# Loading the band tiles of an involution kernel two bands at a time, with smaller rings beside them

## The chip, the cores and the metric

The kernel runs on one core of one Trainium2 chip. The metric is the device time of one execution in microseconds. A core has five engines that run side by side, each in its own order: TensorE (PE in the profile; its weight loads are shown apart as PEld), VectorE (DVE), ScalarE (ACT), GpSimd (POOL) and SyncE (SP). POOL and SP here mostly issue transfers, which the core's 16 DMA engines carry out.

## What is computed

For a batch of 32 images of 256 channels and 32 x 32 pixels, two residual layers:

```
# layer 0
x = x + conv3x3_quantised(group_norm(x)) + bias      # operands and result rounded to fp16
# layer 1: involution, 16 groups of 16 channels, 7 x 7 taps
n = group_norm(x)
y = relu(scale * (w1 @ n) + shift)                   # 64 channels
w = w2 @ y + b2                                      # [16 groups, 49 taps, 32, 32]
x = x + sum over taps k of w[g, k, h, w] * n[g, c, h + k_h - 3, w + k_w - 3]
```

The taps of layer 1 are different at every pixel and are themselves computed. The kernel does the last sum on TensorE: for a block of input pixels it multiplies their channel values by a banded matrix that holds, in each input pixel's row, that pixel's weight in every output pixel in reach.

## The kernel before

**Bands.** An image is cut into K = 4 bands of TR = 8 rows, a band into 2 sides of JC = 16 columns. The 128 partitions of a band tile are the 8 x 16 pixels of one side; each side has its own stretch of 3,528 floats, a window of 22 output columns of 160 floats (16 groups x 10 rows) and a pad. `sums(b, m)` (L508) multiplies one side of one band (m runs over the 8 of an image) with the pixels in 64 matmuls of 64 x 32 (L522) into the PSUM tile `acc`, and `add_windows` (L530) adds the result to x on DVE (L538).

**How a band gets its layout.** `weights(b, r0)` (L403) makes the taps of four image rows on PE (`pw`, L411). `evict` (L424, L435) adds the bias on DVE and writes them into `w_sb`, a ring of RING = 32 output rows in SBUF; `ring_pieces` (L437) cuts the write where the ring or the image ends. `scatter(b, k, part)` (L465) writes the eight rows of a band from `w_sb` to the DRAM array `wd` in seven transfers, one for each horizontal tap (L476): runs of 640 bytes, four transfers in part 0 and three in part 1. `load_bands(b, k)` (L478) reads them back, shifted by a row's offset, into one of NBAND = 3 band tiles: 16 transfers, one for each column j of a side, each with 8 partitions and the two sides of them, runs of 4,512 bytes where nothing is cut off (L497). Columns 0 and 1 go through SP, the other 14 through POOL. Side 1 is stored mirrored, so that both sides have their image edge at j = 0; `backwards` (L277) turns the pixel order of side 1 in xn and y to match. In column 15 the two sides' runs lie side by side and become one.

**Fronts.** `front(b)` (L284) is a generator that does everything before an image's sums: group norm of layer 0 (sums on ACT, L214; grouping on DVE, L224 to L230; mean and squares on ACT), the 3 x 3 convolution in 16-bit (`pc`, L332, 18 matmuls for each of 4 output units), its rounding and residual on DVE (L346, L348), group norm of layer 1, the normalised xn (L273), the 1 x 1 convolution `py` (L377) with its activation to y (L388), and the transposes `pt` of xn (L396), whose copies on ACT (L400) fill one of NPIX = 6 pixel buffers for each band. `py` and `pt` share one PSUM buffer, the single one of the pool `ps_m`. There are two y buffers.

**Order.** The order is written out by hand: the loop at L556 runs over steps n, 16 to an image, and every engine executes its instructions in the order in which the loop emits them. A front advances by one `yield` in each step, except at `yield LATER`, which lets the other fronts go first within the step. Relative to the first sums of image b (step 0), its front starts at step FRONT = -56; `py` comes at step -20, `pt` and copy of its four bands at -14, -12, -10 and -8; `weights` come at every second step from -LEAD = -18; the two parts of a scatter one and two steps after the weights that complete its rows; the load of band k at step 4k - 9; the sums of m at step 2m, their addition to x a step later. About three fronts are in progress at any time, so an engine's queue interleaves several images. Counted within a repeating batch of 16 steps, -20 is the same place as -4, -56 as -8. Within a step the order is: fronts (the oldest image first), sums, addition, store, weights, scatters, load of x, band loads.

The waits between engines follow from the tiles: who overwrites a tile waits for those who read it.

## Time and profile before

| | us |
|---|---|
| three runs | 1348.22, 1356.12, 1360.93 |
| their median | 1356.12 |
| the profiled execution | 1344.24 |
| its span, first to last instruction | 1342.5 |

| engine | busy, us | share | instructions |
|---|---|---|---|
| PE matmul | 1253.6 | 93% | 27,648 |
| PE weight load | 763.7 | 57% | 27,648 |
| DVE | 818.8 | 61% | 2,539 |
| ACT | 733.3 | 55% | 1,731 |
| POOL | 1014.4 | 76% | 1,818 |

The page also shows the traffic: 361.85 MB in all, 270 GB/s over the span. SP's queue moved 229.38 MB and took 56.8% of the 16 engines' time, POOL's 128.28 MB and 33.9%. SP issues 896 scatters of 160 KB, 64 loads of x and 64 stores of 512 KB and 256 band loads; POOL issues 1,792 band loads of mostly 70.5 KB, 4.6 us from issue to landing in the median.

How to read it: the five engines' times overlap, so they don't add up. A share near 100% says only that an engine may be the limit. The chain of waits goes back from the last instruction to what released it, so its shares do add up. A row of a group gives busy time and mean ns of an instruction, then the idle time of its engine just before, with who ended most of it; the idle time of an engine that isn't the limit costs nothing. A matmul's time is modelled. The first sums start at 87.7 us.

### The profile page before, as it was taken

The page shows a single profiled execution, that of the slowest core. Times are in us where ns is not written, and L with a number is a line of the kernel's source. Part 1 is how long each engine was busy: PE and PEld are TensorE (multiplying, and loading weights), DVE is VectorE, ACT ScalarE, POOL GpSimd, SP SyncE. Part 2 cuts the span into 40 slices and gives each one's busy share as a digit, 9 for nine tenths or more (in the row PEclk, how much of TensorE's full clock was granted, in tenths as well). Part 3 has the DMA queues.
Part 4 walks back from the last instruction along what each step waited for, and adds up shares of the span by engine and source line. Part 5 has one row for each costly group of instructions (what it writes and reads, how often), then busy time and mean ns, then how long its engine had stood idle before and what let it go on. Part 6 is the DMA issues. An engine that isn't in the chain of part 4 may idle for free.

```text
span 1342.5 us, 65799 instructions
## 1 busy us (share of the span) xinstructions
PE 1253.6 (93%) x27648; PEld 763.7 (57%) x27648; DVE 818.8 (61%) x2539; ACT 733.3 (55%) x1731; POOL 1014.4 (76%) x1818
## 2 busy tenths in 40 slices
PE   5899999999999999999999999999999999999665
PEld 2356566565555655556655556666555566556454
DVE  3466666565666665656665666766666666666442
ACT  5775656455656556556545655655556564553300
POOL 9067878777787778777778787788777877788785
PEclk9999999999999999999999999999999999999987
DMA  6089999999999999999999999999999999999995
GB/s 228 11 237 295 271 293 293 279 266 281 272 286 282 291 285 270 283 263 280 293 282 283 270 288 282 293 297 296 281 288 275 277 284 290 271 281 266 278 274 166
DMA packets 360724, 361.85 MB, mean 270 GB/s; under 512 B 75056, under 2 KB 304752, under 8 KB 359152
## 3 DMA queue, kind: packets, MB, share of 16 engines
q1 hardware_dynamic: 278512, 229.38, 56.8%
q0 software_dynamic: 81920, 128.28, 33.9%
q8 instruction: 220, 3.60, 1.1%
q14 instruction: 72, 0.59, 0.1%
HBM read 176.60 MB, written 180.76 MB: 266 GB/s over the span
## 4 chain that ended last, share of the span: by engine, by line
PE 60%; DMA 23%; POOL 7%; issue 3%; ACT 3%; DVE 2%; SPq 1%; POOLq 0%; DVEq 0%; ACTq 0%
PE pc L332 25%; PE acc L522 19%; DMA band<-wd 17%; PE pw L411 11%; POOL band L497 7%; DMA wd<-w_sb 6%; PE pt L396 3%; PE py L377 3%; ACT junk L214 1%; SPq L476 1%; DVE w_sb L435 1%; DMA x<-in_x 1%; ACT xn L273 0%; SPq L497 0%; ACT xq L273 0%
## 5 line engine op out<-in xcount | busy, mean ns | idle before, releaser
L497 POOL DMA_DIRECT2D band<-wd x1792 | 980.3, 549 | 315.7 <-DMA band<-wd 182.0
L435 DVE TENSOR_TENSOR w_sb<-pw,late_sb 128x224 f32<-128x224 f32 (+7 forms) x1280 | 330.4, 322 | 419.5 <-PE pw L411 419.2
L332 PE MATMUL pc<-xq,wq 128*128 128x496 f16 (+3 forms) x2304 | 535.2, 379 | 20.3 <-ACT xq L273 18.3
L522 PE MATMUL acc<-band,pixels 64*32 64x190 f32 (+1 forms) x16384 | 426.6, 332 | 51.8 <-DMA band<-wd 42.7
L522 PEld LDWEIGHTS acc<-band,pixels 64*32 64x32 f32 x16384 | 304.7, 107 | 159.7 <-issue 81.1
L332 PEld LDWEIGHTS <-wq 128*128 128x128 f16 x2304 | 206.7, 98 | 316.1 <-issue 102.7
L411 PE MATMUL pw<-late_sb,y 64*32 64x224 f32 (+1 forms) x8192 | 288.9, 333 | 10.8 <-issue 9.4
L538 DVE TENSOR_TENSOR x<-acc,x 128x380 f32<-128x380 f32 (+1 forms) x512 | 262.0, 512 | 32.2 <-PE acc L522 23.2
L411 PEld LDWEIGHTS pw<-late_sb,y 64*32 64x32 f32 x8192 | 186.5, 106 | 38.1 <-issue 21.0
L400 ACT COPY pixels<-pt 128x512 f32<-128x512 f32 x128 | 73.7, 576 | 228.6 <-PE pt L396 228.6
L214 ACT ACTIVATE junk<-x 128x512 f16<-128x512 f32 (+1 forms) x192 | 146.4, 763 | 14.7 <-DVE x L348 12.2
L214 ACT ACTIVATE junk<-x,mean 128x1024 f16<-128x1024 f32 x128 | 147.1, 1149 | 4.3
L245 ACT ACTIVATE s<-back,eps 128x2 f32<-128x2 f32 x64 | 18.9, 296 | 178.6 <-DVE back L230 178.6
L346 DVE TENSOR_SCALAR q<-pc 128x512 f16<-128x512 f32 x128 | 87.2, 681 | 17.6 <-PE pc L332 17.6
L273 ACT ACTIVATE xn<-x,off,rstd 128x512 f32<-128x512 f32 x128 | 96.2, 800 | 0.0
L348 DVE SCALAR_TENSOR_TENSOR x<-q,early_sb,x 128x512 f32<-128x512 f16 x128 | 94.2, 736 | 0.3
L396 PEld LDWEIGHTS pt<-ident,xn 128*128 128x128 f32 x512 | 63.9, 142 | 26.3 <-issue 2.5
L396 PE MATMUL pt<-ident,xn 128*128 128x128 f32 x512 | 78.0, 275 | 0.1
L273 ACT ACTIVATE xq<-x,off,rstd 128x1024 f16<-128x1024 f32 x64 | 75.7, 1227 | 0.0
L235 ACT ACTIVATE mean<-back 128x2 f32<-128x2 f32 x64 | 12.6, 196 | 101.4 <-DVE back L230 101.4
L377 PE MATMUL py<-xn,early_sb 128*64 128x512 f32 x256 | 62.2, 606 | 0.9 <-ACT xn L273 0.9
L224 DVE STREAM_TRANSPOSE across<-sums 128x32 f32<-128x32 f32 x128 | 26.3, 205 | 33.6 <-ACT junk L214 32.4
(40 smaller groups left out, 369.3 us busy)
## 6 DMA issues: line engine op xcount, KB each, us to landing
wd<-w_sb SPq DMA_DIRECT2D x896, 160.0 KB
band<-wd POOLq DMA_DIRECT2D x1664, 70.5 KB, 4.6
x<-in_x SPq DMA_DIRECT2D x64, 512.0 KB
out<-x SPq DMA_DIRECT2D x64, 512.0 KB
band<-wd POOLq DMA_DIRECT2D x128, 60.5 KB, 4.6
band<-wd SPq DMA_DIRECT2D x128, 50.5 KB
band<-wd SPq DMA_DIRECT2D x128, 40.5 KB
band<-in_w SPq DMA_DIRECT2D x2, 1152.0 KB
```

Source lines behind the costliest of these rows:

```text
L214: nc.scalar.activation(junk[:, n0:n1], src[:, h, n0:n1], func, bias=bias, accum_out=self.sums[:, i : i + 1])
L273: nc.scalar.activation(dst, src, AF.Identity, bias=self.off[:, one], scale=self.rstd[:, one])
L332: nc.tensor.matmul(pc.rearrange("p (r c) -> p r c", c=W)[:, r0 - nt * RT : r1 - nt * RT, c0:c1], wq[:, kh, k, mh * P : (mh + 1) * P], xq[: ...
L346: nc.vector.tensor_scalar(q, pc, F16_MAX, -F16_MAX, ALU.min, ALU.max)
L348: nc.vector.scalar_tensor_tensor(xt[:, mh, cols], q, bias_sb[:, mh : mh + 1], xt[:, mh, cols], ALU.add, ALU.add)
L377: nc.tensor.matmul(py[i * CR : (i + 1) * CR], w1_sb[:, kh, :], px[:, :, i], start=kh == 0, stop=kh == CH - 1,)
L396: nc.tensor.transpose(pt[:, i, h * P : (h + 1) * P], xn[:, h, (m + i) * P : (m + i + 1) * P], ident)
L411: nc.tensor.matmul(pws[i][t * TW : (t + 1) * TW, : dj.stop - dj.start, r], y_sb[b % 2][half, (r0 // 2 + r) * W : (r0 // 2 + r + 1) * W], w ...
L435: nc.vector.tensor_tensor(to, of[:, :, d0:d1], bias[:, :, d0:d1], ALU.add)
L497: queue.dma_start(to, src)
L522: nc.tensor.matmul(at[t * TW : (t + 1) * TW, h, :, f - top : l - top], px[p, a, v * GC : v * GC + TW], of[:, :, a, f - top : l - top, v], ...
L538: nc.vector.tensor_tensor(x_at, of, x_at, ALU.add)
```

## The change

- `wd` is laid out as two rows of bands: the eight rows of bands 2q and 2q + 1 lie side by side, 70 columns instead of 38 for each row (SP, ROW).
- `load_bands(b, q, queue, columns)` loads a pair of bands. A transfer of column j takes all four sides of the pair, 32 runs, where no side needs a cut (j = 3 to 12); for the six columns at the edges, side 0 and side 1 have a transfer of their own with 16 runs. Because neighbours now lie side by side in `wd`, what lies beyond an image's edge is cut off in the transfer (cut, end). POOL issues 18 (BY_GPSIMD) and SP four (BY_SYNC) for each pair, in the order of the lists, POOL at step 8q - 9 and SP at 8q - 8.
- The three band tiles become two tiles of a pair each, `halves`, of 13,632 floats; the windows of neighbouring sides follow each other in it.
- Side 1 is no longer mirrored; `backwards` goes.
- One y instead of two; LEAD is 20, so that the first `weights` come in the step of `py`.
- RING is 20 rows instead of 32. `evict` then writes in pieces where the ring ends, and a scatter whose eight rows cross the ring's end becomes two sets of seven transfers of four rows.
- NPIX is 5. HELD moves the copies from `pt` to the pixel buffers: the third comes a step after its `pt`, the fourth three steps after it.
- The scratch for descriptors of POOL's transfers is halved (SCRATCH).

```diff
-ROW = S * WPIX
+BOTH = 2
+SP = BOTH * W + 2 * PAD1
+ROW = SP * WPIX
+STEP = WINC * WB + PAD
+UNITS = BOTH * SIDES
+HALF = (UNITS - 1) * STEP + (JC + PAD1) * WB + PAD
+BY_SYNC = ((0, 0), (15, 1), (1, 0), (14, 1))
+BY_GPSIMD = (
+    (8, None), (4, None), (0, 1), (15, 0), (9, None), (5, None), (1, 1), (14, 0), (10, None),
+    (6, None), (2, 1), (13, 0), (11, None), (7, None), (2, 0), (13, 1), (12, None), (3, None),
+)
+NPIX = 5
+RING = 20
+SCRATCH = 2048
-NBAND = 3
-BY_SYNC = (0, 1)
-ORDER = (0, 4, 8, 12, 2, 5, 9, 13, 3, 1, 6, 10, 14, 7, 11, 15)
-NPIX = 6
-RING = 32
-SCRATCH = 4096
-LEAD = 18
+LEAD = 20
+HELD = (0, 0, 1, 3)
...
-    y_sb = [const.tile([P, N // 2], F32, name=f"y_{i}") for i in range(2)]
-    bands = [const.tile([P, SIDES, WINC * WB + PAD], F32, name=f"band_{i}") for i in range(NBAND)]
-    for t in bands[CH:]:
-        nc.gpsimd.memset(t, 0.0)
+    y_sb = const.tile([P, N // 2], F32, name="y")
+    halves = [const.tile([P, HALF], F32, name=f"bands_{i}") for i in range(2)]
+    parts = [halves[0][:, : HALF // 2], halves[0][:, HALF // 2 :]]
+    zeros = halves[1]
+    for i in range(8):
+        nc.gpsimd.memset(zeros[:, i * HALF // 8 : (i + 1) * HALF // 8], 0.0)
-    wd = dram.tile([H, S, WPIX], F32, name="wd")
+    wd = dram.tile([K // BOTH, TR, SP, WPIX], F32, name="wd")
...
             yield
             to = xn[:, h].rearrange("p (k d r j) -> p d k r j", d=SIDES, r=TR, j=JC)
             at = xt[:, h].rearrange("p (k r d j) -> p d k r j", d=SIDES, r=TR, j=JC)
-            gn.apply(h, [(to[:, 0], at[:, 0]), (to[:, 1], backwards(at[:, 1]))])
+            gn.apply(h, [(to[:, d], at[:, d]) for d in range(SIDES)])
         yield from stages(2)
 
         py = ps_m.tile([P, NT], F32, tag="m", name="py")
...
                     start=kh == 0,
                     stop=kh == CH - 1,
                 )
-        to = y_sb[b % 2].rearrange("p (k r d j) -> p d k r j", k=K, d=SIDES, j=JC)
+        to = y_sb.rearrange("p (k r d j) -> p d k r j", k=K, d=SIDES, j=JC)
         of = py.rearrange("p (k d r j) -> p d k r j", k=K, d=SIDES, j=JC)
         for d in range(SIDES):
-            at = of[:, d]
-            nc.scalar.activation(to[:, d], backwards(at) if d else at, AF.Relu, bias=bn_shift, scale=bn_scale)
+            nc.scalar.activation(to[:, d], of[:, d], AF.Relu, bias=bn_shift, scale=bn_scale)
         yield from stages(5)
 
         for m in range(0, M, 2):
...
                     nc.tensor.transpose(
                         pt[:, i, h * P : (h + 1) * P], xn[:, h, (m + i) * P : (m + i + 1) * P], ident
                     )
+            yield from stages(HELD[m // 2])
             to = pixels[(b * M + m) // 2 % NPIX].rearrange("p i a (v c) -> p (i a) v c", c=GC)
             nc.scalar.copy(to[:, :, ::2], pt.rearrange("p i (a v c) -> p (i a) v c", v=2, c=GC))
-            yield
+            yield from stages(1 - HELD[m // 2])
 
     def weights(b, r0):
 
...
         at = (b * H + k * TR) % RING
         for dj in range(part, K1, 2):
             t, e = divmod(dj, 2)
-            to = bass.AP(
-                tensor=wd.tensor,
-                offset=wd.offset + k * TR * ROW + dj * WPIX + (K1 - 1 - dj) * WB,
-                ap=[[WPIX, TW], [ROW, TR], [1, WB]],
-            )
-            rows = w_sb[t * TW : (t + 1) * TW, e, at : at + TR]
-            nc.sync.dma_start(to, rows.rearrange("p s a r v -> p s (a r v)"))
-
-    def load_bands(b, k):
-
-        band = bands[(b * K + k) % NBAND]
-        side = WINC * WB + PAD
-        for i, j in enumerate(ORDER):
-            cut = max(0, PAD1 - j)
-            n = (K1 - cut) * WB + PAD
+            n = min(TR, RING - at)
+            for r, rows, s in ((0, n, at), (n, TR - n, 0)):
+                if rows == 0:
+                    continue
+                to = bass.AP(
+                    tensor=wd.tensor,
+                    offset=wd.offset
+                    + ((k // BOTH * TR + r) * SP + k % BOTH * W + dj) * WPIX
+                    + (K1 - 1 - dj) * WB,
+                    ap=[[WPIX, TW], [ROW, rows], [1, WB]],
+                )
+                of = w_sb[t * TW : (t + 1) * TW, e, s : s + rows]
+                nc.sync.dma_start(to, of.rearrange("p s a r v -> p s (a r v)"))
+
+    def load_bands(b, q, queue, columns):
+
+        for j, d in columns:
+            units, side, step = (UNITS, 0, 1) if d is None else (BOTH, d, SIDES)
+            cut = max(0, PAD1 - j) if d == 0 else 0
+            end = min(K1, JC + PAD1 - j) if d == 1 else K1
+            n = (end - cut) * WB + PAD
             src = bass.AP(
                 tensor=wd.tensor,
-                offset=wd.offset + k * TR * ROW + (j + PAD1) * WPIX + cut * WB,
-                ap=[[ROW - V, TR], [(W - 1 - 2 * j) * WPIX - cut * WB, SIDES], [1, n]],
+                offset=wd.offset + (q * TR * SP + side * JC + j + PAD1) * WPIX + cut * WB,
+                ap=[[ROW - V, TR], [step * JC * WPIX, units], [1, n]],
             )
-            to = band[j::JC]
+            to = halves[(b * K // BOTH + q) % 2][j::JC]
             to = bass.AP(
                 tensor=to.tensor,
-                offset=to.offset + (j + cut) * WB,
-                ap=[to.ap[0], [side + (JC - 1 - 2 * j - cut) * WB, SIDES], [1, n]],
+                offset=to.offset + side * STEP + (j + cut - PAD1) * WB,
+                ap=[to.ap[0], [step * STEP, units], [1, n]],
             )
-            queue = nc.sync if j in BY_SYNC else nc.gpsimd
             queue.dma_start(to, src)
 
     def windows(b, m):
...
 
         k, d = divmod(m, SIDES)
         j0 = 0 if d else PAD1
-        band = bands[(b * K + k) % NBAND][:, d]
+        band = halves[(b * K + k) // BOTH % 2]
+        unit = (k % BOTH * SIDES + d) * STEP - PAD1 * WB
         px = pixels[(b * K + k) % NPIX][:, d]
         for h in range(CH):
             for v in range(2):
                 for g, at, top, f, l in windows(b, m):
                     p = slice(g * KP, (g + 1) * KP)
-                    of = band[p, V * g * XR + j0 * WB : V * g * XR + (j0 + WINI) * WB]
+                    of = band[p, unit + V * g * XR + j0 * WB : unit + V * g * XR + (j0 + WINI) * WB]
                     of = of.rearrange("p (j a r v) -> p j a r v", a=A, r=WIN, v=V)
                     for t in range(T):
                         a = h * T + t
...
             if i == 0 and b > 1:
                 x_tiles[b] = load_x(b)
 
-            b, i = due(n, 3 - 4 * NBAND)
-            if b is not None and i % 4 == 0:
-                load_bands(b, i // 4)
+            for lag, queue, columns in ((-9, nc.gpsimd, BY_GPSIMD), (-8, nc.sync, BY_SYNC)):
+                b, i = due(n, lag)
+                if b is not None and i % 8 == 0:
+                    load_bands(b, i // 8, queue, columns)
 
 
 _OUT = (B, C, H, W)
```

More of the change, by code (lines that the diff above doesn't have):

```diff
@@ L156, in tile_quant_conv_then_involution @@
     for kh in range(CH):
-        wf = bands[kh].rearrange("p d n -> p (d n)")[:, : K0 * K0 * C].rearrange("p (k c) -> p k c", c=C)
+        wf = parts[kh][:, : K0 * K0 * C].rearrange("p (k c) -> p k c", c=C)
         nc.sync.dma_start(wf, w0[kh * P : (kh + 1) * P])
@@ L181, in tile_quant_conv_then_involution @@
     for col, cols, at, n in (
-        (0, S, K1 * WB, PAD),
+        (0, SP, K1 * WB, PAD),
         (PAD1, PAD1, 0, PAD1 * WB),
-        (W, PAD1, (K1 - PAD1) * WB, PAD1 * WB),
+        (BOTH * W, PAD1, (K1 - PAD1) * WB, PAD1 * WB),
     ):
@@ L188, in tile_quant_conv_then_involution @@
             offset=wd.offset + col * WPIX + at,
-            ap=[[ROW, H], [WPIX, cols], [1, n]],
+            ap=[[ROW, K // BOTH * TR], [WPIX, cols], [1, n]],
         )
-        nc.sync.dma_start(to, bands[NBAND - 1][:H, 0, :n].unsqueeze(1).to_broadcast([H, cols, n]))
+        nc.sync.dma_start(to, zeros[: K // BOTH * TR, :n].unsqueeze(1).to_broadcast([K // BOTH * TR, cols, n]))
     def quantize_weights(kh):
         nc.vector.tensor_scalar(wq[:, kh], staged[kh], F16_MAX, -F16_MAX, ALU.min, ALU.max)
-        nc.gpsimd.memset(bands[kh], 0.0)
         if kh == CH - 1:
+            for t in parts:
+                nc.gpsimd.memset(t, 0.0)
             nc.gpsimd.memset(w_sb, 0.0)
@@ L275, in tile_quant_conv_then_involution @@
     LATER = 1
-    def backwards(at):
-        step, n = at.ap[-1]
-        return bass.AP(tensor=at.tensor, offset=at.offset + step * (n - 1), ap=[*at.ap[:-1], [-step, n]])
     CONV = (9, 0, 9, 0)
@@ L412, in weights @@
                         pws[i][t * TW : (t + 1) * TW, : dj.stop - dj.start, r],
-                        y_sb[b % 2][half, (r0 // 2 + r) * W : (r0 // 2 + r + 1) * W],
+                        y_sb[half, (r0 // 2 + r) * W : (r0 // 2 + r + 1) * W],
                         w2_sb[half, dj],
```

## The prediction

> **What bounds the kernel now.** I read the page's wait chain first (the chain that ended last, by share), then the costliest groups with what ended their idle time, then busy times window by window, then the timelines of two places.
>
> ```profile
> PE 60%; DMA 23%; POOL 7%; issue 3%; ACT 3%; DVE 2%; SPq 1%; POOLq 0%; DVEq 0%; ACTq 0%
> PE pc L332 25%; PE acc L522 19%; DMA band<-wd 17%; PE pw L411 11%; POOL band L497 7%; DMA wd<-w_sb 6%; PE pt L396 3%; PE py L377 3%; ACT junk L214 1%; SPq L476 1%; DVE w_sb L435 1%; DMA x<-in_x 1%; ACT xn L273 0%; SPq L497 0%; ACT xq L273 0%
> ...
> L497 POOL DMA_DIRECT2D band<-wd x1792 | 980.3, 549 | 315.7 <-DMA band<-wd 182.0
> ```
>
> TensorE carries the chain, but a quarter of it is the band path: POOL issuing loads and their landing. POOL spends 549 ns on each of 1,792 loads and another 182 us waiting for earlier ones, because every POOL load waits for the one eight before it (so stand the semaphores in the program). (980 + 182) / 128 bands = 9.1 us, against 9.9 us that a band lasts: POOL is almost as tight as PE.
>
> The windows, one per batch, cut at the end of py, tell the floor:
>
> ```profile
> 757.50:797.00 39.50, 38.47 (x872) 23.37 (x879) 25.28 (x79) 22.77 (x55) 31.67 (x58) 1.00 0.97 286
> 797.00:834.90 37.90, 37.90 (x869) 23.37 (x871) 25.29 (x79) 22.71 (x55) 28.76 (x54) 1.00 0.98 289
> 834.90:873.00 38.10, 38.10 (x874) 23.26 (x880) 25.28 (x79) 22.83 (x55) 29.09 (x54) 1.00 0.98 289
> 873.00:910.90 37.90, 37.90 (x871) 23.13 (x874) 25.28 (x79) 22.71 (x55) 31.47 (x59) 1.00 0.98 294
> ```
>
> The columns are length, busy PE, PEld, DVE, ACT, POOL, clock, DMA share, GB/s. Three batches in a row have PE busy all the time: 38.0 us is PE's floor. Over 195.5 to 1227.7 us 26 batches take 39.7 us each, so 1.7 us a batch is lost to stalls. The DMA engines are busy 0.96 to 0.98 throughout, so they stand close behind.
>
> The end is another stage: PE's timeline there shows four bands that each wait for their load, 9 us apart:
>
> ```profile
> 1308.49 5.21 PE L522 MATMUL acc<-band,pixels 64*32 64x133 f32 x128 [3.79 <-DMA band<-wd]
> 1316.77 4.55 PE L522 MATMUL acc<-band,pixels 64*32 64x190 f32 x128 [3.07 <-DMA band<-wd]
> 1325.02 5.32 PE L522 MATMUL acc<-band,pixels 64*32 64x190 f32 x128 [3.70 <-DMA band<-wd]
> ```
>
> With no convolution left, the band path alone sets the pace.
>
> **What the Trainium skill says.** "DMA: Bandwidth & Descriptors", Anatomy of one DMA, calls descriptor generation small: many descriptors can be emitted before the added cost shows. The trace agrees within its span: the loads of column 15, whose two sides are contiguous (8 runs of 9 KB), and those of 16 runs all take about 0.55 us (547 minimum, 547 median, 681 maximum over the line). No run here shows 32. "Perfetto Trace Analysis", DMA Instruction — SWDGE, says that the reported end is the end of descriptor generation, not of the movement; here 0.55 us against 4.6 us to landing. The first page, Issuing engines are not separate DMA queues, says that SP's and POOL's transfers share the same 16 engines; GB/s staying near 285 in every window agrees. So a transfer regrouped is not a byte saved.
>
> **The change, part by part.** A batch is 16 steps; step numbers count from the batch's first sums.
>
> *Band loads.* Per pair POOL issues 18 transfers for 28 (10 of 32 runs, 8 of 16), SP four as before; bytes and runs are the same. At 0.55 us: 9.9 us a pair instead of 15.3, so POOL falls from 980 to about 630 us. If the price went with the runs, the ten would take 1.1 us and nothing be saved; I take 0.55. Larger transfers land later; with eight in flight and, I estimate, 6 to 7 us to landing (4.6 us measured for half the data), a pair needs 18 x 6.5 / 8 = 15 us. The two buffers let it start when the last sums before step -9 end: from 859.3 us in the timeline, the sums that need it come at 881.4, a window of 22 us. 15 us and a landing fit, so I take the band stalls in the middle as gone: at most 1.7 us x 29 batches = **-49 us**. The other end is 0: the same engines must move the same bytes.
>
> *Pixels: five buffers, the last copy held three steps.* This is the step that costs. The copy (L400) of a batch's last pair moves from step -8 to step -5, behind the squares of another batch in ACT's order, and py (L377, step -4) needs the same PSUM buffer as pt. Before, py waited for xn alone and the squares ended during or after py:
>
> ```profile
> 870.93 1.15 ACT L214 ACTIVATE junk<-x,mean 128x1024 f16<-128x1024 f32 x1
> ...
> 872.21 1.15 ACT L214 ACTIVATE junk<-x,mean 128x1024 f16<-128x1024 f32 x1
> ...
> 873.35 1.00 ACT L388 ACTIVATE y<-py,bn_shift,bn_scale 128x256 f32<-128x256 f32 x2
> ```
>
> py ran from 871.05. Will ACT be earlier? Its chain began at 863.07 after 2.96 us of waiting for pt of step -8; that wait goes, since the copy in that place is now one whose pt is 2 steps old. Then DVE sets the squares: eviction from 864.96 (1.28), x L348 (0.74), two acc adds (1.1), group (0.7) = 868.6; mean 0.2, squares 2.4, copy 0.6 = 871.9. PE stalls 0.85 us. In two of five batches this eviction has 14 instructions for 4 (below), +0.67, so on average +0.26: **1.1 us x 31 = +34 us**. Range 0 (ACT earlier) to 2 us a batch. Behind py on PE stand that step's sums and pw, so everything shifts. The copy's own wait, for the sums that free its buffer at step -6, is over by 868.4 and costs nothing; the third copy, now at -9, waits for sums that end at 859.3 and goes at 859.9, before ACT's chain.
>
> *Ring of 20 rows.* Evictions that cross its end are split: 1,280 become 2,180. From 4 in 1.28 us and the edge groups' 8 smaller in 1.33 us, an instruction costs 0.067 us beside 1.13 ns an element, so 900 x 0.067 = 60 us of DVE. DVE is at 61% and waits 419 us for pw; that covers it, apart from the step above. The scatters rise from 896 to 1,078 (one band in five splits in two); SP waits 161 us on evictions, which covers most of 182 x 0.5 = 91 us. New is a wait: an eviction overwrites rows whose scatter was released four steps (two evictions) earlier. By the timeline an eviction ends at 861.5 and the second after it starts at 869.4: 8 us. In SP's timeline the seven scatters it releases go out by 870.2 (the last four of one row and the three of the next, two band loads between), and the chain of waits shows 4.0 us to landing at another place (635.2): 12 us or more. Without the band loads between (SP now loads after both bands) and their waits, I estimate 9 us. Behind the waiting eviction on DVE stand x L348, acc adds and q, for which ACT and PE wait; PE needs pw's buffer only 1.9 us after an eviction now ends. So 1 us is hidden and only split bands bite: **0.3 us x 31 = +9 us**; at 12 us it is the slow rival.
>
> *LEAD 20, one y.* Weights, evictions and scatters move two steps ahead. On SP a batch's first scatters now pass the loads of x, which stand between their two parts; SP waits 77 us for stores before those loads, so the second part can come 2 to 3 us late, counted in the range of the ring. On POOL nothing is passed: loads alone are queued there. On PE, pw now follows py within its step. y ends 1.05 us after py if ACT is free (it is, the copy came before), and the sums between take 1.3: hidden, barely. The memsets of new sizes lie under the first convolutions. The first load (71.7 us, first sums at 87.7) needs two bands scattered instead of one, one eviction later (4.7 us in the timeline), less the two steps' lead: **+2 us**, estimated, 0 to 5. A halved descriptor scratch: nothing, unless POOL waits more; then the band gain shrinks towards 0. Dropping the mirroring changes only ACT's reading direction: nothing.
>
> *The end.* Five and three-quarter pairs at 17.8 us now, 15 us or less after (18 x 6.5 / 8): **-15 us**, 0 to -25.
>
> Sum: -49 + 34 + 9 + 2 - 15 = -19. The profiled execution took 1344.2 us, 0.9% under the median 1356.1: 1325 on its own scale, **1337** on the median's.
>
> **The rivals.** (a) *Slower: the small ring.* DVE waits for scatters, because bursts of larger loads starve them: beyond 10.5 us from eviction to landing (8 + 0.6 + 1.9) PE stalls. At 12 us for two bands a batch and more for split ones it is about 2.4 us a batch beside the 1.1: 41.5 us, +52 + 2 - 15 = +39, or 1395. For it: the 12 us above and a DMA share of 0.97. Against: no band loads between, and PE's slack. (b) *The DMA engines are the bound.* 11.1 MB a batch at 285 GB/s is 39 us; then the middle gains nothing, the gate hides in that time, and only the end gains: 1344 - 13 = 1331, or 1343. Against: batches of 37.9 us at 294 GB/s. (c) *The gate does not bite*, because ACT and DVE run earlier: -49 + 5 - 13 = -57, 1298. (d) *The change doesn't do what it says*: the price goes with the runs, POOL stays at 15.3 us a pair, the stalls stay and the gate hides mostly in them: +10, 1366. Against: the equal 0.55 us at 8 and 16 runs.
>
> **How the numbers follow.** Forecast 0.41 (1318 to 1352), (a) 0.29, (b) 0.12, (c) 0.14, (d) 0.04. About 1% is what a measurement can tell from no change, so the bounds are 1342.6 and 1369.7. Faster takes three quarters of the forecast, (c) and half of (b): 0.51. Within 1%: the rest of both and half of (d), 0.18. Slower: (a) and half of (d), 0.31. The range of 1300 to 1393 leaves out half of (c) and somewhat under half of (a), with the unknown prices inside it.
>
> **What would show it.** POOL near 0.55 us a load and under 650 us busy; no "acc <- DMA bands" in the middle's waits; py waiting for ACT pixels by about 1 us a batch (new row); DVE evictions waiting for DMA wd<-w_sb little; the last bands closer than 9 us. The forecast is wrong if evictions wait for DMA by more than 60 us, if POOL's mean rises to 0.8 us, or if the batch takes over 39.7 us.

## The result, and the profile after

| | before | after |
|---|---|---|
| median, us | 1358.53 (4 runs, 1348.22 to 1361.09) | 1681.50 (4 runs, 1672.27 to 1685.48) |
| ratio | 1 | 1.241 [1.235, 1.246] |
| profiled execution, span, us | 1342.5 | 1683.6 |
| a batch in the middle (py to py), us | 39.7 | 50.2 |
| first sums, us | 87.7 | 103.8 |
| last py to the end, us | 84.0 | 92.5 |
| mean granted PE clock | 0.982 | 0.908 |
| POOL busy, us | 1014.4 | 649.5 |

The prediction said 1337. The change costs 323 us, nearly all of it in the middle: about 10.5 us in each batch. After's page, the chain of waits and the rows of the band loads and evictions:

```profile
PE 36%; DMA 32%; DVE 13%; SPq 9%; ACT 6%; issue 3%; POOL 0%; DVEq 0%; POOLq 0%; ACTq 0%
DMA wd<-w_sb 30%; PE pc L338 13%; PE pw L417 10%; PE acc L534 9%; SPq L488 7%; DVE w_sb L441 7%; ACT junk L225 3%; DVE x L550 2%; PE py L383 2%; DMA bands<-wd 1%; PE pt L401 1%; DVE x L354 1%; SPq L508 1%; DVE back L241 1%; ACT xq L284 1%
...
L508 POOL DMA_DIRECT2D bands<-wd x1152 | 614.0, 538 | 1017.6 <-DMA wd<-w_sb 376.8
L441 DVE TENSOR_TENSOR w_sb<-pw,late_sb 128x16 f32<-128x16 f32 (+9 forms) x2180 | 397.2, 250 | 699.0 <-DMA wd<-w_sb 399.1
```

The band path has left the chain (bands<-wd 1%, POOL 0%), as hoped. In its place stands the writing of the bands: the scatters 30%, their issue on SP 7%, the evictions 7%. The waits view of after names the waiting engine, what it waits for, the total, the number and the longest:

```profile
DVE w_sb L441 <- DMA wd<-w_sb: 399.1, 98, 10.2
...
PE pw L417 <- DVE w_sb L441: 236.0, 51, 10.3
```

An eviction waits until the ring's rows have been scattered, and PE waits for the eviction. One such place in three timelines of after; DVE, SP and PE:

```profile
612.80 1.97 DVE L441 TENSOR_TENSOR w_sb<-pw,late_sb 128x64 f32<-128x64 f32 x14
...
617.84 1.28 DVE L441 TENSOR_TENSOR w_sb<-pw,late_sb 128x224 f32<-128x224 f32 x4 [1.48 <-PE pw L417]
...
623.83 0.39 DVE L441 TENSOR_TENSOR w_sb<-pw,late_sb 128x224 f32<-128x224 f32 x1 [2.43 <-DMA wd<-w_sb]
634.21 0.98 DVE L441 TENSOR_TENSOR w_sb<-pw,late_sb 96x224 f32<-96x224 f32 x3 [9.99 <-DMA wd<-w_sb]
```

```profile
615.71 2.43 SPq L488 DMA_DIRECT2D wd<-w_sb  x4
618.24 2.21 SPq L114 DMA_DIRECT2D x<-in_x  x2
620.56 18.60 SPq L488 DMA_DIRECT2D wd<-w_sb  x10
```

```profile
617.67 2.08 PE L338 MATMUL pc<-xq,wq 128*128 128x496 f16 x9
...
634.75 2.32 PE L417 MATMUL pw<-late_sb,y 64*32 64x224 f32 x32 [8.33 <-DVE w_sb L441]
637.00 3.61 PE L338 MATMUL pc<-xq,wq 128*128 128x496 f16 x9
...
650.96 1.94 PE L383 MATMUL py<-xn,early_sb 128*64 128x512 f32 x8 [1.36 <-ACT pixels L406]
```

The eviction of 612.80 completes a band. SP sends the four scatters of part 0, then the loads of x (1 MB), then the three of part 1 (the last line of SP merges these three, issued by 623.0, with the next band's seven, from 634.9 on). The second eviction after it writes over the same rows: its first piece, at 623.83, needs part 0 and waits 2.4 us; the piece of 96 partitions needs part 1, which stands behind x, and waits 10 us more. PE stands 8.3 us, and its next nine matmuls take 3.61 us, where such nine took 2.08 before: a second price of the stall. Over the whole kernel PE is busy 1346.2 us instead of 1253.6 with the same 27,648 matmuls, so about 93 of the 341 us between the two profiled spans are slower matmuls; PE's waits for evictions are 236. At 650.96 py waits for the held pixel copy; that gate was predicted.

### The profile page after: what moved, and what is told of

Same layout as the page of the kernel before. It is cut to its first block, busy times and chain, and to the rows that moved or that the text cites. A ratio compares the mean times of both kernels' runs of the same rounds, so it can differ in the third digit from the quotient of the medians.

```text
span 1683.6 us, 65695 instructions
## 1 busy us (share of the span) xinstructions
PE 1346.2 (80%) x27648; PEld 779.2 (46%) x27648; DVE 882.5 (52%) x3439; ACT 738.9 (44%) x1731; POOL 649.5 (39%) x1184
## 3 DMA queue, kind: packets, MB, share of 16 engines
q1 hardware_dynamic: 281232, 229.20, 50.2%
## 4 chain that ended last, share of the span: by engine, by line
PE 36%; DMA 32%; DVE 13%; SPq 9%; ACT 6%; issue 3%; POOL 0%; DVEq 0%; POOLq 0%; ACTq 0%
DMA wd<-w_sb 30%; PE pc L338 13%; PE pw L417 10%; PE acc L534 9%; SPq L488 7%; DVE w_sb L441 7%; ACT junk L225 3%; DVE x L550 2%; PE py L383 2%; DMA bands<-wd 1%; PE pt L401 1%; DVE x L354 1%; SPq L508 1%; DVE back L241 1%; ACT xq L284 1%
## 5 line engine op out<-in xcount | busy, mean ns | idle before, releaser
L508 POOL DMA_DIRECT2D bands<-wd x1152 | 614.0, 538 | 1017.6 <-DMA wd<-w_sb 376.8
L441 DVE TENSOR_TENSOR w_sb<-pw,late_sb 128x16 f32<-128x16 f32 (+9 forms) x2180 | 397.2, 250 | 699.0 <-DMA wd<-w_sb 399.1
L338 PE MATMUL pc<-xq,wq 128*128 128x496 f16 (+3 forms) x2304 | 573.7, 399 | 23.0 <-ACT xq L284 19.8
L417 PE MATMUL pw<-late_sb,y 64*32 64x224 f32 (+1 forms) x8192 | 330.8, 355 | 245.3 <-DVE w_sb L441 236.0
L534 PE MATMUL acc<-bands,pixels 64*32 64x190 f32 (+1 forms) x16384 | 418.9, 329 | 30.9 <-DMA bands<-wd 10.9
L338 PEld LDWEIGHTS <-wq 128*128 128x128 f16 x2304 | 216.3, 102 | 354.5 <-issue 156.9
L534 PEld LDWEIGHTS acc<-bands,pixels 64*32 64x32 f32 x16384 | 296.8, 106 | 139.5 <-issue 97.0
L417 PEld LDWEIGHTS pw<-late_sb,y 64*32 64x32 f32 x8192 | 195.6, 111 | 308.1 <-issue 277.8
L225 ACT ACTIVATE junk<-x 128x512 f16<-128x512 f32 (+1 forms) x192 | 146.4, 762 | 32.5 <-DVE x L354 29.8
L383 PE MATMUL py<-xn,early_sb 128*64 128x512 f32 x256 | 63.4, 617 | 31.7 <-ACT pixels L406 31.7
L393 ACT ACTIVATE y<-py,bn_shift,bn_scale 128x256 f32<-128x256 f32 x64 | 32.6, 560 | 67.6 <-PE py L383 67.6
```

The source lines that it names most:

```text
L225: nc.scalar.activation(junk[:, n0:n1], src[:, h, n0:n1], func, bias=bias, accum_out=self.sums[:, i : i + 1])
L338: nc.tensor.matmul(pc.rearrange("p (r c) -> p r c", c=W)[:, r0 - nt * RT : r1 - nt * RT, c0:c1], wq[:, kh, k, mh * P : (mh + 1) * P], xq[: ...
L383: nc.tensor.matmul(py[i * CR : (i + 1) * CR], w1_sb[:, kh, :], px[:, :, i], start=kh == 0, stop=kh == CH - 1,)
L417: nc.tensor.matmul(pws[i][t * TW : (t + 1) * TW, : dj.stop - dj.start, r], y_sb[half, (r0 // 2 + r) * W : (r0 // 2 + r + 1) * W], w2_sb[ha ...
L441: nc.vector.tensor_tensor(to, of[:, :, d0:d1], bias[:, :, d0:d1], ALU.add)
L508: queue.dma_start(to, src)
```

## The experiments

Ratios are to the kernel before, run on the same chip in the same session; x_late, x_pool and the kernels before with 20, 22 and 23 rows have two runs each, the others four or more. The line numbers in a timeline are those of its own kernel, a few lines off from before or after. "Evictions wait" is the row above, of the profiled execution.

### Is it the order in SP's queue, or the ring?

x_late is after with the loads of x a step later, behind both parts; x_pool is after with the loads of x, but for the first two images, on POOL's queue:

```diff
-LOAD = -63
+LOAD = -62
```
```diff
...
-                x_tiles[b] = load_x(b)
+                x_tiles[b] = load_x(b, nc.gpsimd)
```

> The changed kernel with one number different: the load of x comes one step later (LOAD -62), so that it stands behind both scatter parts of an image's first band in SP's queue instead of between them. Theory Q (queue order): the stall of about 10 us a batch is the second scatter part waiting behind 1 MB of x in one queue; with x behind it the evictions' wait for DMA wd<-w_sb falls from 399 us to under 120, PE's wait for evictions from 236 us to under 60, and the time to 1350 to 1420 us. Rival B (bandwidth): the larger POOL transfers fill the DMA engines and the scatters land late wherever they stand; the evictions still wait over 300 us and the time stays above 1580. Rival R (the 20-row ring is too short by itself): between the two, 1450 to 1580.

> The changed kernel with the loads of x (all but the first two images) issued by POOL at the same step instead of SP. The same bytes move at nearly the same time, only not in SP's queue. Theory Q: as with the later load, 1350 to 1420 us, evictions wait under 150 us for scatters. Rival B: the engines are shared all the same, so the scatters land as late as now and the time stays above 1580. Rival R: 1450 to 1580.

before_ring20 is the kernel before with after's ring and after's cuts of the scatters, and nothing else; before_pix5 is the kernel before with after's pixel buffers and late copies:

```diff
-RING = 32
+RING = 20
...
```
```diff
-NPIX = 6
+NPIX = 5
+HELD = (0, 0, 1, 3)
...
```

> The kernel before with the ring of 20 rows alone (evictions and scatters split where it ends; bands, loads, LEAD 18, y and pixels as before). In the trace of before the scatters of an image's first band land 12.6 us after the eviction that releases them, the second 10.2, the third 10.9, and the second eviction after begins 8.6 us after. Theory Q with a short ring: DVE waits 4 us for the first band and 1.6 to 2.3 for the others, PE has 1.9 us of slack, so it loses 2 to 3 us a batch and some clock: 1400 to 1450 us. Rival B (it takes the pair loads' bursts): under 1385. Rival R: over 1480.

> The kernel before with five pixel buffers and the held copies alone. The prediction's gate: py waits for the last pixel copy by about 1.1 us a batch, which partly lies in stalls that the middle has anyway (1.7 us a batch): PE py waits for ACT pixels 20 to 40 us in all, time 1360 to 1392 (ratio 1.00 to 1.025). If the gate doesn't bite, under 5 us of such waits and a ratio within 0.5% of 1.

| run | median, us | ratio | evictions wait, us |
|---|---|---|---|
| x_late | 1571.25 | 1.161 [1.153, 1.170] | 280.0 |
| x_pool | 1553.57 | 1.148 [1.138, 1.158] | 280.5 |
| before_ring20 | 1563.89 | 1.156 [1.151, 1.161] | 372.0 |
| before_pix5 | 1360.19 | 1.006 [1.004, 1.008] | none |

Taking x out of the way saves 110 to 128 us of the 323 and no more; both times lie where rival R put them. The ring of 20 rows in a kernel that is otherwise the one before costs 211 us (before took 1352.7 in that session), far more than the 50 to 100 that I had expected. Its DVE timeline has no single wait of 10 us as in after, but several of 2.5 to 4.7 us in a batch:

```profile
723.76 0.98 DVE L435 TENSOR_TENSOR w_sb<-pw,late_sb 96x224 f32<-96x224 f32 x3 [2.49 <-DMA wd<-w_sb]
...
736.22 0.98 DVE L435 TENSOR_TENSOR w_sb<-pw,late_sb 96x224 f32<-96x224 f32 x3 [4.72 <-DMA wd<-w_sb]
...
748.41 1.06 DVE L435 TENSOR_TENSOR w_sb<-pw,late_sb 96x128 f32<-96x128 f32 x6 [4.67 <-DMA wd<-w_sb]
```

The late copies alone cost 0.6%, near the edge of what can be measured.

### The ring: its length, or the pieces it is cut into?

Kernels as before_ring20, with RING = 22 and RING = 23. The eviction of r0 = 8j writes up to row 8j + 6. With 20 and 22 rows it lands on the band whose scatter was released two evictions earlier (8j + 6 - 22 = 8j - 16, that band's first row); with 23, only on the one before it, and the nearest is three evictions old.

> The kernel before with a ring of 22 rows instead of 32 (evictions and scatters cut where the ring ends). Distance theory: with 22 rows the eviction of weights r0 = 8j still reaches row 8j + 6 - 22 = 8j - 16, the first row of the band whose scatter was released two evictions (four steps) earlier, so it waits as with 20 rows: ratio to before 1.10 to 1.17, DVE evictions waiting for wd<-w_sb 250 to 400 us. Rival, the number of pieces: the cuts at the ring's end (more instructions on DVE, more scatters on SP) cost the time; then 22 and 23 rows, which have the same cuts in nearly the same number, take the same time.

> As the kernel with 22 rows, but 23. Distance theory: one row more moves the reuse by r0 = 8j to row 8j - 17, of the band before; the nearest scatter in the way was then released three evictions (six steps, 13 to 14 us at before's pace) earlier, and scatters of before land 10 to 13 us after the eviction that releases them: ratio 0.99 to 1.05, evictions waiting for wd<-w_sb under 80 us. Rival, the number of pieces: ratio within 0.02 of that of 22 rows, both over 1.08.

| rows | evictions issued | evictions wait, us | ratio |
|---|---|---|---|
| 20 | 2,180 | 372.0 | 1.156 |
| 22 | 2,136 | 237.6 | 1.097 [1.086, 1.108] |
| 23 | 2,058 | 124.6 | 1.054 [1.043, 1.064] |

The pieces hardly change, so they don't make the difference between these three: DVE's busy time is 884, 880 and 873 us. The time follows the wait. What the pieces cost by themselves is at most the 5.4% that is left with 23 rows. But the step between 22 and 23 is less sharp than expected: with 23 rows there are still 60 waits of up to 6.5 us, so a distance of three evictions doesn't always suffice either. And 22 rows wait less than 20, though both reach the same band two evictions on; why was not followed up. With 32 rows, in before, no eviction waits for a scatter.

### After's pairs, with a ring that fits

24 rows keep bands whole and the reuse at least three evictions away. There is no room for it beside the pairs, so these kernels keep the first half of the convolution's weights alone and use it for both halves of the channels; sizes and counts of instructions stay.

```diff
-RING = 20
+RING = 24
-    wq = const.tile([P, CH, K0 * K0, C], F16, name="wq")
+    wq = const.tile([P, 1, K0 * K0, C], F16, name="wq")
...
-                        wq[:, kh, k, mh * P : (mh + 1) * P],
+                        wq[:, 0, k, mh * P : (mh + 1) * P],
```

pair_ring24_late has LOAD = -62 too. pair_ring24_sq has mean and squares of layer 0 one step later, so that the held copy stands ahead of the squares on ACT:

```diff
+        yield
         yield LATER
         gn.means()
         gn.squares(xt)
-        yield from stages(3)
+        yield from stages(2)
```

> The kernel after with a ring of 24 rows, where bands start at multiples of eight and no scatter is cut; the memory for it comes from keeping only the first half of the weights of the 3 x 3 convolution and using it for both halves of the input channels (the second half is left out; same instructions, same sizes). Everything else is after's: loads of pairs, one y, five pixel buffers, late copies, the loads of x between the two parts of a scatter. Distance theory: the ring's waits were all of the loss, so evictions wait for wd<-w_sb under 80 us and the ratio to before is 0.97 to 1.04, with py waiting for pixel copies 30 to 60 us. Rival: bursts of 32-run loads starve the scatters or the loads of x hold up SP's queue whatever the ring; then evictions still wait over 150 us and the ratio stays over 1.07.

> As the kernel with pairs and 24 rows (the second half of the convolution's weights left out), with the mean and squares of layer 0 one step later, so that the held pixel copy stands ahead of the squares in ACT's order. Gate theory (the copy behind the squares makes py wait): py's wait for pixels falls under 12 us and the time falls by 15 to 40 us against the kernel with pairs and 24 rows. Rival: the gate lies beside a PE that would wait for something else anyway (bands, evictions, pixels of sums); then py's row falls and the time stays within 8 us.

> The kernel with pairs and 24 rows (the second half of the convolution's weights left out), with LOAD -62 instead of -63: the loads of x stand behind both parts of the first band's scatters in SP's queue. Queue theory: the 131 us that evictions still wait for wd<-w_sb come from the part that stands behind the loads of x, so they fall under 40 us and the time falls by 25 to 70 us, ratio 1.08 to 1.11; the rest is another cause. Rival (the 24 rows are still too short by themselves): evictions keep over 90 us and the time stays within 15 us.

| run | median, us | ratio | evictions wait, us |
|---|---|---|---|
| pair_ring24 | 1527.06 | 1.132 [1.123, 1.142] | 130.9 |
| pair_ring24_sq | 1533.13 | 1.137 [1.128, 1.146] | 145.5 |
| pair_ring24_late | 1530.63 | 1.128 [1.123, 1.134] | 8.5 |

My theory fell here: the ring was not all of the loss. In pair_ring24_late the evictions' wait is gone, and the time is the same. In its place PE has a wait that has no row in before and 3.9 us in after; POOL waits for scatters as well, about as long as in after (376.8):

```profile
POOL bands L509 <- DMA wd<-w_sb: 354.1, 30, 44.8
...
PE acc L535 <- DMA wd<-w_sb: 100.0, 38, 6.5
```

The sums don't read the scatters; they read the loads, and the releaser named is a scatter that ended at about the same time. What happens is seen by laying two timelines of pair_ring24 side by side, POOL's and PE's:

```profile
669.63 5.29 POOL L509 DMA_DIRECT2D bands<-wd  x10 [11.75 <-DMA wd<-w_sb]
...
678.72 2.16 POOL L509 DMA_DIRECT2D bands<-wd  x4 [0.19 <-issue]
690.37 5.29 POOL L509 DMA_DIRECT2D bands<-wd  x10 [9.49 <-DMA out<-x]
```

```profile
654.81 0.95 PE L418 MATMUL pw<-late_sb,y 64*32 64x224 f32 x32
...
671.64 0.96 PE L418 MATMUL pw<-late_sb,y 64*32 64x224 f32 x32
...
686.91 1.50 PE L535 MATMUL acc<-bands,pixels 64*32 64x133 f32 x55 [1.13 <-DMA wd<-w_sb]
...
709.36 1.61 PE L535 MATMUL acc<-bands,pixels 64*32 64x190 f32 x64 [2.10 <-DMA wd<-w_sb]
```

The weights at 654.81 complete the pair's second band. By the packets of the trace its last scatter lands at 668.2; POOL, idle for 11.75 us, starts the pair's 18 loads at 669.6 and issues until 680.9; the last lands at 685.8, and the sums of its first band, 12 steps after the weights, start at 686.9, 1.1 us late. From weights to sums 32 us are needed; 12 steps of before's batch are 12/16 x 39.7 = 29.8. The image's other pair has 14 steps, 34.7 us at that pace, and needs 37.7 (weights at 671.64, sums at 709.36, 2.1 us late). In before a band's sums come 14 to 16 steps after the weights that complete it, and its loads are 16 instead of 22.

### Latency from weights to sums

pair_stale24 keeps everything of pair_ring24 except that wait, on POOL and on SP, which loads four columns of a pair: `wd` has four pairs of bands, and each load reads the pair before the one it should, whose scatters landed long ago. Bytes, runs and queues are the same, but the sums use old weights. pair_stale24_late has LOAD = -62 as well. before_lead16 goes the other way, in the kernel before: weights two steps later, so that single bands have after's 12 steps.

```diff
...
-                offset=wd.offset + (q * TR * SP + side * JC + j + PAD1) * WPIX + cut * WB,
+                offset=wd.offset + (max(b * K // BOTH + q - 1, 0) % K * TR * SP + side * JC + j + PAD1) * WPIX + cut * WB,
...
```
```diff
-LEAD = 18
+LEAD = 16
```

> The kernel with pairs and 24 rows, but wd has four pairs of bands and each load reads the pair before the one it should (the sums use old weights; besides, the second half of the convolution's weights is left out). Bytes, runs, queues and counts are the same; only the wait of a pair's loads for the scatters of its own second band is gone. Latency theory: in after the loads of a pair come 3 steps after the weights that complete its second band and its sums 12 steps after them (14 to 16 for a band in before), and eviction, scatter, 18 issues and landing take all of that; without it sums no longer wait for wd<-w_sb (100 us before), POOL's wait for wd<-w_sb is gone, and the time falls by 40 to 110 us, ratio 1.05 to 1.10, what is left being the loads of x between the parts. Rival (the loads' own bursts or the evictions are what is left): time within 20 us of the kernel with pairs and 24 rows, ratio over 1.115.

> Both: loads of the pair before, and LOAD -62 (old weights are used; the second half of the convolution's weights is left out). If ring, order of the loads of x, and latency of a pair are the three causes of the loss, nothing is left of it: ratio 0.95 to 1.01, batches of 38 to 40 us. If the pair loads harm in another way (burst against scatters, gate at py, one y), the ratio stays over 1.03.

> The kernel before with LEAD 16 instead of 18: weights, evictions and scatters two steps later, loads where they are, so that the first band's sums come 12 steps after the weights that complete it, as in after, and its loads 3 steps after. Latency theory: eviction 1.5 to 2, scatter 10 to 13, issue of 14 loads 8 to 9, landing 4.6 us are 25 to 29 us, against 12 steps of 2.45 us = 29: just short or just enough for single bands, so sums wait for loads by 0 to 2 us a batch more: ratio 1.00 to 1.04, and POOL waits for wd<-w_sb more than in before. Rival (the distance from weights to sums doesn't matter, the size of a pair's burst does): ratio 0.997 to 1.003, no row of sums waiting for wd<-w_sb.

| run | median, us | ratio |
|---|---|---|
| pair_stale24 | 1386.81 | 1.022 [1.016, 1.028] |
| pair_stale24_late | 1358.57 | 1.001 [0.999, 1.004] |
| before_lead16 | 1527.29 | 1.125 [1.120, 1.131] |

The wait for a pair's own scatters is worth 140 us (1527.06 to 1386.81, on two chips on which before differs by 5; with the loads of x moved in both it is 172 us on one chip, 1530.63 to 1358.57), more than the 110 that I had expected at most. The order of the loads of x, which gave nothing while that wait set the pace, is worth another 28 once it is gone. With all three causes away, the loss is gone. And two steps of lead less, in the kernel before, cost 12.5%, as much as after's pairs do: a loss of that size doesn't need pairs. I had expected at most 4%. Its waits name the loads:

```profile
PE acc L522 <- DMA band<-wd: 151.7, 38, 7.3
```

The shorter distance isn't all that changes, though. SP has loads of bands in its queue too, and with two steps less they stand close behind the scatters that they read, so SP waits for them, and the next band's scatters wait behind. SP's own waits, in before and then in before_lead16:

```profile
SPq L497 <- DMA wd<-w_sb: 20.9, 36, 1.2
```

```profile
SPq L497 <- DMA wd<-w_sb: 374.5, 133, 5.8
```

An image's third band, for whose loads PE waits most, has its first scatter issued 2.5 us after its eviction ends, where in before it goes out at once, and lands 12.6 us after it for 10.9 (medians). The same row has 201.3 us in pair_ring24 and 17.9 in pair_stale24. So part of what is called latency here is SP's queue held up by its own loads; no run takes those loads out of SP's queue while loads still wait for their own scatters, and how much of the loss is theirs stays open.

### Why nothing is left over

pair_stale24_late has the gain that was hoped for (no band stalls, half of POOL idle) and yet only equals before. Candidates: the gate at py, the DMA engines, PE. In the first of these the squares move as in pair_ring24_sq; pair_less drops SP's four loads of a pair (`BY_SYNC = ()`, those columns keep old values; 3.3% of the bytes and, by the packets of pair_stale24_late, 3.0% of the DMA engines' time); pair_less_sq does both. All are made from pair_stale24_late and leave out the same things.

> As the kernel with 24 rows, loads of the pair before and LOAD -62 (old weights; the second half of the convolution's weights left out), with the mean and squares of layer 0 one step later, so that the held pixel copy stands ahead of them in ACT's order. Gate theory: now that nothing else stops PE, py's wait for pixels (18.5 us on PE, 31 on its weight loads) is on the path; it falls under 8 us and the time by 15 to 35 us, ratio 0.975 to 0.99. Rival (something else sets the batches of 40.8 us): time within 8 us of the kernel without the move, ratio over 0.994.

> As the kernel with 24 rows, loads of the pair before and LOAD -62 (old weights; the second half of the convolution's weights left out), and without SP's four loads of a pair: the columns 0 and 1 of side 0 and 14 and 15 of side 1 keep old values. That is 11.6 of 361.8 MB, 3.2%. DMA theory (the 16 engines, busy 1.00 in its batches of 40.0 us, are what is left): the batch shrinks by 1.0 to 1.3 us until the gate or PE's 38.0 stops it, 39.0 at the least with the gate at py, so the time falls by 20 to 40 us, ratio 0.97 to 0.987. Rival (PE or a wait that the trace doesn't show sets 40.0): time within 8 us of the kernel with the loads.

> As the one before it (the same things left out), with the mean and squares of layer 0 one step later. DMA theory: with 3.2% fewer bytes PE can come near its 38.0 us, and the gate, which hid in the DMA engines' time, now counts: 5 to 20 us less than with the gate. Rival: within 5 us of it.

| run | median, us | ratio | batch, us |
|---|---|---|---|
| pair_stale24_late | 1358.57 | 1.001 [0.999, 1.004] | 40.0 |
| pair_stale24_late_sq | 1363.25 | 1.006 [1.004, 1.009] | 40.1 |
| pair_less | 1352.44 | 1.001 [0.998, 1.003] | 39.9 |
| pair_less_sq | 1352.93 | 1.000 [0.998, 1.003] | 39.9 |

Neither the move nor the fewer bytes gain anything: both theories missed. The move is no clean test of the gate: py's wait for pixels falls from 18.5 us to 0.2, but pw then waits 14.1 us for y instead of 4.2. Windows of 200 us from the middle, pair_stale24_late and then pair_less (length, busy PE, PEld, DVE, ACT, POOL, clock, DMA share, GB/s):

```profile
700.00:900.00 200.00, 194.88 (x4328) 118.64 (x4326) 134.48 (x500) 116.52 (x276) 96.87 (x182) 1.00 1.00 280
```

```profile
700.00:900.00 200.00, 193.58 (x4396) 118.01 (x4374) 133.41 (x496) 116.60 (x272) 96.57 (x182) 1.00 0.98 271
```

The bytes fell, the DMA engines' busy share a little less. From 300 to 1100 us PE is busy 96% of the time in both and 97% in before (771.9, 769.1 and 777.8 of 800 us). What makes a batch last 1.9 us over PE's best 38.0 isn't settled. It isn't the band stalls: pair_stale24_late has none from 300 to 1200 us, some 23 batches, and before, whose batch is 1.7 us over, only

```profile
PE acc L522 <- DMA band<-wd: 13.9, 11, 2.7
```

### A kernel that beats both?

Three edits of the kernel before that the runs pointed to: more of the last images' loads on SP (before_tail: five columns in the last three images, eight in bands 1 to 3 of the last), a third column on SP throughout (before_sync3), two steps more of lead (before_lead20).

```diff
...
-            queue = nc.sync if j in BY_SYNC else nc.gpsimd
+            queue = nc.sync if j in by_sync(b, k) else nc.gpsimd
```
```diff
-BY_SYNC = (0, 1)
+BY_SYNC = (0, 1, 15)
```
```diff
-LEAD = 18
+LEAD = 20
```

> The kernel before, with more of the last images' band loads on SP: five columns instead of two in the last three images, eight of 16 in bands 1 to 3 of the last one. If POOL's issue and its eight in flight set the pace of the last bands (four waits of 2.8 to 3.8 us on band<-wd from 1308 us on), most of these waits go: 6 to 18 us less, ratio 0.987 to 0.996. Rival: the DMA engines' own time sets it; then 0.998 to 1.003, and the earlier images' scatters on SP may even wait behind the added loads (up to 1.01).

> The kernel before with column 15 on SP too (three columns, POOL 13 loads a band instead of 14). If POOL's issue is what leaves the 1.7 us a batch of stalls in the middle and the 9 us between the last bands, POOL falls by 70 us and the time by 5 to 20 us, ratio 0.985 to 0.997. Rival (SP's queue then holds up the scatters, or the DMA engines are what is left): 0.998 to 1.02.

> The kernel before with LEAD 20 instead of 18: weights, evictions and scatters two steps earlier, in the step of py; two y, ring of 32 rows and single bands as before. Latency theory: LEAD 16 cost 12.5%, so 18 has little to spare; if the sums' waits for bands in the middle (about 1 us a batch) come from scatters that land late, two more steps take them away: 8 to 25 us less, ratio 0.982 to 0.994. Rival (at 18 steps the latency is already covered, and POOL's rate or PE itself is left): 0.996 to 1.01, the same waits for band<-wd in the middle, perhaps a new small wait of pw for y.

They gave 1.003 [1.000, 1.005], 1.010 [1.005, 1.014] and 1.008 [1.006, 1.011]. None gains. In before_tail PE still waits for the last bands, for one of them longer than for any in before:

```profile
1344.06 5.00 PE L528 MATMUL acc<-band,pixels 64*32 64x190 f32 x128 [12.08 <-DMA band<-wd]
```

LEAD 20 gains nothing where LEAD 16 loses 12.5%: at 18 the latency is just covered. A kernel with pairs, 24 rows, all of the convolution's weights and more lead was not tried; memory for the rows, and for a sixth pixel buffer that an earlier front would want, is lacking.

## Why the prediction was wrong

**The step that failed first** is the ring: "Without the band loads between ... I estimate 9 us" from eviction to landing, of which "1 us is hidden and only split bands bite: 0.3 us x 31 = +9 us". In the timelines of after the eviction that completes the band ended at 614.8, and by the packets of the trace the last of its scatters landed at 633.5: 18.7 us, of which some 10 are the loads of x (part 0 had landed at 623.0). The other three bands of an image, with no x between their parts, land 6.5, 10.2 and 14.4 us after their evictions there (medians): two of three over the 9. The chain of waits has one scatter of 11.77 us there (622.32 on), while the 9 us rested on one of 4.0. Within the very kernel before, by the trace's packets, scatters land 10.2 to 12.6 us (medians of the four bands) after the eviction that releases them: the number was there to be measured, and I took one value from the chain and then reduced it. The term's size was 211 us in before_ring20. Rival (a) named the mechanism, with its 12 us, but as 2.4 us a batch, where before_ring20's batches are 46.6 for 39.7: 6.9 us. It counted waits alone; before_ring20 has 127 us of PE waiting for evictions and 93 us of slower matmuls.

**The loads of x** between the two parts were seen ("can come 2 to 3 us late") and mis-sized: 10 us in the timeline, 110 us in x_late. The Trainium skill, "DMA: Bandwidth & Descriptors", Queues, rings and completion order, says that each DMA engine consumes a ring's descriptors in order; the two timelines agree, as the part behind 1 MB of x came 10 us after the part ahead of it. The prediction had counted the delay of the loads' issue, and not the time that their 1 MB takes in the queue.

**"15 us and a landing fit, so I take the band stalls in the middle as gone"** failed in its start, not in its 15 us. I let the loads start when their buffer came free, -9. They start when the second band has landed. The issue was as priced (11 us in the timeline of pair_ring24, a landing 5.5), but the sum that decides, weights to sums, was never made: 32 us against 29.8. In after it doesn't show, since the ring makes a batch 50.2 us, and 12 steps of that are 37.7. That fits causes that don't add (211, 110 and 140 us against 323 in all): where one sets the pace, another is hidden in part.

**The gain of 49 us** was too large by most of it even so. The waits for bands in the middle did go (one of 10.9 us left in all of after), but they were 13.9 us over 23 batches, 0.6 us a batch; I had put the whole 1.7 us to them.

**The gate** was right in place and size: py waits 31.7 us in 29 places in after, 1.1 us each, as worked out. As a loss of 34 us it was wrong: before_pix5, where py waits 18.8 us, has 8 us, and taking it away gave nothing three times (pair_ring24_sq, pair_stale24_late_sq, pair_less_sq), though each time some of it came back as pw's wait for y.

**POOL's price** was right: 536 ns for a load of 32 runs and 541 for one of 16, and 649.5 us busy. So (d) is out.

**The start** was +16 us, not +2, and not for the reason given. In after's timeline the first sums follow the convolution without a wait for bands; what stands ahead of them is pw waiting for y, py waiting for the held copy, and evictions:

```profile
55.30 0.98 PE L417 MATMUL pw<-late_sb,y 64*32 64x224 f32 x32 [3.06 <-ACT y L393]
...
76.68 0.68 PE L417 MATMUL pw<-late_sb,y 64*32 64x224 f32 x2 [3.45 <-DVE w_sb L441]
...
91.15 3.34 PE L383 MATMUL py<-xn,early_sb 128*64 128x512 f32 x8 [2.99 <-ACT pixels L406]
...
103.83 1.41 PE L534 MATMUL acc<-bands,pixels 64*32 64x133 f32 x60
```

before_lead20, with single bands, starts its sums at 95.8, which is half of the 16. **The end** took 73.5 us from the last py in pair_stale24_late, 10.5 less than before, but its loads don't wait for their own scatters; pair_ring24, whose loads do, took 83.6 and after 92.5. So the -15 wasn't shown.

**(b)**, the DMA engines as the bound, gets no support from pair_less. Of the signs that were to tell against the forecast two came true: evictions waiting for DMA 399 us for a limit of 60, batches of 50.2 for 39.7.

## What to carry to other kernels

Before a buffer is shrunk or a transfer made larger, add up the whole loop from the engine that makes the data to the one that uses it, in measured landing times at full load, and compare it with the steps between them; here two steps of lead fewer cost 12.5%, and two more gained nothing. Look at what stands in the same queue: a small transfer behind 1 MB landed 10 us later, and a load that waits for its data holds up what is queued behind it. A saving on an engine that isn't the bound is worth only the waits on the bound that name it, so count those waits, and not the difference to the best batch.

## What was not expected of the hardware

- A stalled PE costs twice: after 8.3 us of waiting, nine matmuls of 128 x 128 by 496 took 3.61 us for 2.08, and over all of after PE was busy 7.4% longer for the same matmuls, at a mean clock of 0.908 for 0.982. The Trainium skill, "TensorE: Matmul & The Clock Gate", What's actually happening, says that the clock falls to half after an idle window of about 3.4 us; the trace agrees in kind.
- A POOL issue costs the same 0.53 to 0.55 us whether it moves 70 KB in 16 runs or 141 KB in 32, and landing rises only from 4.6 us to 5.3 (in after, where loads of 70 KB take 5.1 themselves).
- A DMA share of 1.00 didn't mean that the DMA engines set the time: with 3.3% fewer bytes it fell from 1.00 or 1.01 to 0.98 or 0.99, the rate from 280 to about 271 GB/s, and the time stayed within 0.4%.
